# Macaron Mamba block: z's products in a stream of their own, one PSUM bank and one gate per token tile, buffers and ranks set anew

## The chip, the cores and the metric

The kernel runs on one NeuronCore of a Trainium2 chip. The metric is the time of one execution on the device in microseconds (us); the engines are TensorE (PE), VectorE (DVE), ScalarE (ACT), GpSimd (POOL) and SyncE (SP, which here only issues DMAs). All times are of this core.

## The reference

x holds 4096 tokens of 1024 channels in float32. Three residual steps follow each other: half a feed-forward layer with a ternary weight, a Mamba layer, and the same feed-forward layer again.

```python
def _L0_ffn_ref(x, weight, bias):
    scale = jnp.mean(jnp.abs(weight))
    w_t = jnp.clip(jnp.round(weight / (scale + EPS)), -1.0, 1.0)
    w_ste = weight + jax.lax.stop_gradient(w_t * scale - weight)
    return jnp.einsum('bsi,oi->bso', x, w_ste) + bias

def _mamba(x, W_in, conv_w, conv_b, W_xproj, W_dt, b_dt, A_log, Dskip, W_out):
    u, z = jnp.split(x @ W_in.T, 2, axis=-1)
    up = jnp.pad(u, ((0, 0), (K - 1, 0), (0, 0)))
    u = jax.nn.silu(conv_b + sum((conv_w[:, k] * up[:, k:k + L, :] for k in range(K))))
    x_dbl = u @ W_xproj.T                      # 64 for dt, 16 for B, 16 for C
    dt = jax.nn.softplus(dt_r @ W_dt.T + b_dt)
    # for each token: h = exp(dt * A) * h + dt * B * u ;  y = sum over the 16 states of h * C
    y = (y + u * Dskip) * jax.nn.silu(z)
    return y @ W_out.T

x = x + 0.5 * _L0_ffn_ref(_layernorm(x), weight, bias)
x = x + _mamba(_layernorm(x), ...)
x = x + 0.5 * _L0_ffn_ref(_layernorm(x), weight, bias)
```

## The kernel before

**Tiling.** The tokens go through in 16 chunks (`NC`) of 256 (`T`), each of two token tiles of 128 (`TT`). The 1024 channels are 8 blocks of 128; a half is four blocks, and the recurrence handles a chunk half by half: 32 halves, each with a skip term (n = -1) and 16 states (n = 0 to 15). That makes 544 "products", of which 512 come from VectorE.

**One state.** GpSimd multiplies u·dt by the state's B (line 934, a tile h) and adds the entering state to the first column (941). ScalarE makes the decays exp(dt·A), four instructions of 255 columns (913), into two PSUM tiles da. VectorE runs two scans over 512 columns (966), then multiplies by C (978, a tile p). TensorE sums over the states: eight transposes of 128 columns that accumulate p into the PSUM tile y (998). y is one tile of two banks, one for each token tile, and there is one such tile (line 210). After the 16th state the gate (1015) multiplies the whole of y by silu(z) on VectorE, 1024 columns at once, and only then can the next half's skip term be summed into y.

**One chunk.** `front` is one sequential generator: load x, feed-forward (`ffn`: layer norm, transposes 425, products with the ternary weight split in two parts 497, residual 476), layer norm, u's products (629), convolution and silu (574, 581), the product with W_xproj (641), `delta` of the first half (710, softplus 722), and then the next chunk. z's products (677) stand in `rest`, behind `delta` of the second half. `back` does the rest of a chunk: transposes of the gated y (752), W_out (760), residual (731), and the second feed-forward layer. `last` is `back` for the last chunk. Weights of u, z and W_out stream through five buffers; each of these streams asks for some of them ahead (`ahead`: 2, 3 and 3).

**What sets the order.** The order on every engine is made when the program is built. Each piece of work is a Python generator, a stream with a rank, that yields wishes (engine, duration, earliest time). The loop in `Streams.run` gives the instruction to the stream that can start first, and to the lower rank in a tie. The durations are constants in the code; the chip then executes each engine's queue strictly in that order, waiting on semaphores. So ranks (`DECAY`, `ENTER`, ... in lines 57 and 58), assumed latencies (`ADDED` for the bias DMA, 5000 ns for a weight) and numbers of buffers change the order of instructions, and so which engine waits for which. The eight PSUM banks are three free ones (`banks`), three for decays (`decays`) and the two of y.

Of the kernel before, what the change touches and what calls it, by code (L numbers as in the profile page):

```python
# [38 lines left out]
P = 128  # L39
# [13 lines left out]
REACH = 160  # L53
ISSUE, ADDED = 950, 6000
SWITCH = 1300

DECAY, ENTER, SUM, PREPARE, RECUR, GATE = 5, 1, 1, 0, 2, 2
FFN_A, NORM, U_PART, CONV, DELTA, OUT, FFN_C = 0, 0, 3, 0, 0, 2, 3

# [114 lines left out]
def macaron_mamba_kernel(  # L174
# [34 lines left out]
    decays = buffers(3, [P, 2, T], "da", pool_=psum)  # L209
    ys = buffers(1, [P, TT, OH], "y", pool_=psum)  # L210
    xs = buffers(6, [P, D], "x")
    xts = buffers(2, [P, NB, T], "xT")
# [128 lines left out]
    def streamed(load, n, ahead, rank):  # L341

        queue = []

        def fill():
            for i in range(n):
                yield lambda: 0 if len(queue) < ahead else INF
                w = yield from weights.take()
                load(i, w)
                queue.append((order.now + 5000, w))  # L350

        order.spawn(fill(), rank)
        return queue
# [26 lines left out]
    def stats(c, at, tiles=range(TT)):  # L380
# [4 lines left out]
        rstd, shift, less = ln[:, 28:30][:, some], ln[:, 32:34][:, some], ln[:, 36:38][:, some]  # L385
        xn = {}
        for t in tiles:
            xn[t] = yield from tmps.take()
# [50 lines left out]
    def ffn(c, which, rank, at, tiles=range(TT)):  # L439
# [32 lines left out]
        def residual(t, cols, pf, at_):  # L472
# [3 lines left out]
            nc.vector.scalar_tensor_tensor(xt, pf, hscl, xt, ALU.mult, ALU.add)  # L476
            if (*key, t) != ("a", 0, 1):
                banks.put(pf, end)
            ready["ffn", key, t, cols.start] = end
# [35 lines left out]
    def as_weights_come(key, parts, residual, rank):  # L515

        for t in range(TT):
            yield from when("parts", key, t)
        y = yield from ys.take()
        groups = {(1, h): y[:, h, :] for h in range(2)}  # L520
        for h in range(2):
            groups[0, h] = yield from banks.take()
        for k in range(NB):
            yield from when("wf", k)
# [12 lines left out]
        for t in range(TT):  # L537
            los.put(parts[t][0], end)
            his.put(parts[t][1], end)
        for h in range(2):  # L540
            end = yield from when("ffn", key, 1, h * OH)
        ys.put(y, end)

# [40 lines left out]
    def front():  # L584
        for c in range(NC):
# [32 lines left out]
            for pair in range(NB // 2):  # L618
# [4 lines left out]
                for j in range(2):  # L623
# [9 lines left out]
                    weights.put(w, end)  # L633
            yield DELTA
            px = yield from banks.take()
            for half in range(2):
                at = yield from when("u", c, half)
                end = yield pe(2 * HB * T * FULL)
                for b in range(HB):
                    k = half * HB + b  # L640
                    nc.tensor.matmul(
                        px[:NXD, :T], wx[:, k, :], u[c, half][:, b, :], start=(k == 0), stop=(k == NB - 1)
                    )
            xd[c] = yield from xds.take()
            end = yield act(T, end + REACH)
            nc.scalar.copy(xd[c][RANK:NXD, 1, :], px[RANK:NXD, :T])
            for j in range(2):
                end = yield act(T)
                nc.scalar.copy(xd[c][j * RANK : (j + 1) * RANK, 0, :], px[:RANK, :T])
            banks.put(px, end)  # L650
            bc_dram[c] = dram.tile([NST, 2, T], F32, tag="bc", name=f"bcd_{c}")
            for j in range(2):
                part_ = slice(RANK + j * NST, RANK + (j + 1) * NST)
                nc.sync.dma_start(bc_dram[c][:, j, :], xd[c][part_, 1, :])
            ready["bc", c] = end + 2500
# [80 lines left out]
    def turned(c, half, yT):  # L736
# [188 lines left out]
    def enter():  # L925
        for c, half, n in items:
# [61 lines left out]
    def summed():  # L988
        for c, half, n in items:
            yield from when("product", c, half, n)  # L990
            if n < 0:
                y = yield from ys.take()
            p = product.pop((c, half, n))
            end = yield pe(D * TURN)

            for t in range(TT):
                for b in range(HB):
                    nc.tensor.matmul(  # L998
                        y[:, t, b * P : (b + 1) * P],
                        p[:, b, t * P : (t + 1) * P],  # L1000
                        ident,
                        start=(n < 0 and b == 0),
                        stop=(n == NST - 1 and b == HB - 1),
                        is_transpose=True,
                        skip_group_check=True,
                    )
            products.put(p, end)
            if n + 1 == NST:
                order.spawn(gate(c, half, y, end + REACH), GATE)

    def gate(c, half, y, at):
        yield from when("z", c, half)
        z = sz[c, half]
        end = yield dve(1170, at)
        nc.vector.tensor_tensor(flat(z), flat(y), flat(z), ALU.mult)
        ys.put(y, end + REACH)
        ready["gate", c, half] = end + REACH

# [80 lines left out]
```

## Time and profile before

| what | value |
|---|---|
| median of 3 runs | 2726.5 us (2725.86 to 2727.03) |
| the profiled execution | 2725.84 us |
| its span, first to last instruction | 2724.1 us |
| mean granted TensorE clock | 0.983 |
| PE busy | 2568.1 us (94%) |
| DVE busy | 2288.3 us (84%) |
| ACT busy | 2001.4 us (73%) |
| POOL busy | 1815.6 us (67%) |
| DMA | 410.82 MB, mean 151 GB/s |

Busy is the time in which an engine has at least one instruction in work. Matmuls overlap in TensorE's pipeline: eight transposes that follow each other begin 0.87 us after the eight before them began, though each is listed with some 0.27 us. A float32 matmul with 256 columns is listed as two records, one transpose or one product of the feed-forward layer as one. The granted clock is the share of its pulses that TensorE was let have; it is below 1 where TensorE was idle before. An idle engine is named with the instruction that ended its wait.

### The profile page before, as it was taken

What the parts mean: (1) busy time and instruction counts of PE and PEld (TensorE: products, weight loads), DVE (VectorE), ACT (ScalarE), POOL (GpSimd) and SP (SyncE); (2) the same over time, 40 slices, a digit from 0 to 9 for tenths busy, and PEclk for the clock granted to TensorE, in tenths of its full rate; (3) what the DMA queues carried; (4) which work ended last, traced back from release to release, by engine and by line L of the source; (5) the groups of instructions that cost most, each with busy time, mean ns of one, the idle gap of its engine ahead of it and who ended that gap; (6) DMA issues with size and microseconds to landing.
All of it is one profiled execution on the core that took longest, in us unless ns stands there. A gap on an engine that the chain in (4) does not pass through costs nothing. (4 is left out here: it accounts for less than half of the span.)

```text
span 2724.1 us, 41050 instructions
## 1 busy us (share of the span) xinstructions
PE 2568.1 (94%) x14082; PEld 2199.6 (81%) x14082; DVE 2288.3 (84%) x2404; ACT 2001.4 (73%) x4202; POOL 1815.6 (67%) x1657
## 2 busy tenths in 40 slices
PE   5797989999999999999999999999999999999988
PEld 4686878888788787888878788887888878788866
DVE  4498898978899798888879799898889879788883
ACT  3678677787877778777787877778787777877662
POOL 0367767766677585767757577686767857577761
PEclk9897999999999999999999999999999999999999
DMA  4443536455454545546554454655545554554533
GB/s 158 146 130 103 168 106 216 132 166 149 134 173 140 179 151 153 155 129 184 166 162 144 140 167 132 182 162 155 153 140 167 159 172 146 150 157 133 182 85 109
DMA packets 218553, 410.82 MB, mean 151 GB/s; under 512 B 19172, under 2 KB 85860, under 8 KB 218344
## 3 DMA queue, kind: packets, MB, share of 16 engines
q1 hardware_dynamic: 209128, 374.65, 43.3%
q0 software_dynamic: 9216, 33.56, 6.8%
q8 instruction: 110, 1.80, 0.3%
q14 instruction: 99, 0.81, 0.1%
HBM read 390.82 MB, written 17.31 MB: 150 GB/s over the span
## 5 line engine op out<-in xcount | busy, mean ns | idle before, releaser
L934 POOL TENSOR_TENSOR h<-u,bc 128x1024 f32<-128x1024 f32 x512 | 1223.2, 2389 | 421.7 <-ACT da L913 171.1
L966 DVE TENSOR_TENSOR_SCAN h<-da,h 128x512 f32<-128x512 f32 x1024 | 1207.7, 1206 | 125.6 <-ACT da L913 99.7
L913 ACT ACTIVATE da<-dt,pr 128x255 f32<-128x255 f32 x2048 | 938.6, 473 | 61.9 <-DVE h L966 32.9
L978 DVE TENSOR_TENSOR p<-h,bc 128x1024 f32<-128x1024 f32 x512 | 658.7, 1286 | 6.6 <-PE y L998 6.4
L998 PE MATMUL y<-ident,p 128*128 128x128 f32 x4352 | 572.5, 278 | 79.5 <-DVE p L978 61.1
L998 PEld LDWEIGHTS y<-ident,p 128*128 128x128 f32 x4352 | 503.9, 143 | 151.5 <-DVE p L978 95.4
L629 PE MATMUL bank<-xT,weight 128*128 128x256 f32 x2048 | 474.7, 382 | 11.4 <-ACT u L562 8.6
L677 PE MATMUL bank<-weight,xT 128*128 128x256 f32 x2048 | 474.7, 380 | 9.2 <-DMA weight<-in_w_in 9.2
L760 PE MATMUL bank<-weight,u 128*128 128x256 f32 x2016 | 467.3, 381 | 2.2 <-DMA weight<-in_w_out 1.9
L629 PEld LDWEIGHTS bank<-xT,weight 128*128 128x128 f32 x2048 | 378.6, 190 | 69.9 <-ACT u L562 21.3
L677 PEld LDWEIGHTS bank<-weight,xT 128*128 128x128 f32 x2048 | 380.2, 191 | 56.7 <-ACT da L913 9.9
L760 PEld LDWEIGHTS bank<-weight,u 128*128 128x128 f32 x2016 | 370.9, 191 | 47.2 <-DMA weight<-in_w_out 2.1
L949 ACT COPY state<-h 128x4 f32<-128x4 f32 x512 | 99.2, 194 | 292.5 <-DVE h L966 287.5
L941 POOL TENSOR_TENSOR h<-h,over 128x4 f32<-128x4 f32 x512 | 262.5, 513 | 25.2
L497 PE MATMUL bank<-wf,lo 128*128 128x512 f32 x976 | 252.3, 400 | 3.7 <-DVE lo L455 2.4
L574 DVE SCALAR_TENSOR_TENSOR u<-up,pr,u 128x256 f32<-128x256 f32 x384 | 206.4, 570 | 55.2 <-ACT u L562 42.6
L497 PE MATMUL bank<-wf,hi 128*128 128x512 f32 x976 | 245.8, 394 | 0.0
L497 PEld LDWEIGHTS bank<-wf,lo 128*128 128x128 f32 x976 | 177.7, 188 | 48.4 <-issue 4.0
L497 PEld LDWEIGHTS bank<-wf,hi 128*128 128x128 f32 x976 | 181.7, 188 | 43.0 <-issue 4.3
L865 POOL TENSOR_TENSOR over<-pr,dt 128x64 f32<-128x64 f32 x32 | 24.9, 778 | 211.3 <-ACT dt L722 211.3
L476 DVE SCALAR_TENSOR_TENSOR x<-bank,hscl,x 128x512 f32<-128x512 f32 x124 | 91.2, 737 | 71.9 <-PE bank L497 71.8
L425 PE MATMUL bank<-ident,tmp 128*128 128x128 f32 x756 | 115.9, 285 | 27.1 <-ACT tmp L409 23.4
(98 smaller groups left out, 2125.0 us busy)
## 6 DMA issues: line engine op xcount, KB each, us to landing
bc<-bcd SPq DMA_DIRECT2D x512, 256.0 KB, 3.7
weight<-in_w_out SPq DMA_DIRECT2D x128, 512.0 KB, 5.1
weight<-in_w_in SPq DMA_DIRECT2D x128, 512.0 KB, 3.7
weight<-in_w_in SPq DMA_DIRECT2D x256, 256.0 KB, 4.2
x<-hbias POOLq DMA_DIRECT2D x64, 512.0 KB, 7.9
x<-in_x SPq DMA_DIRECT2D x32, 512.0 KB, 7.3
out<-x SPq DMA_DIRECT2D x30, 512.0 KB, 4.9
weight<-in_w_ffn SPq DMA_DIRECT2D x5, 512.0 KB, 7.4
```

Of the source, the lines that this page charges most:

```text
L425: nc.tensor.matmul(pt[:, j * P : (j + 1) * P], xn[:, k * P : (k + 1) * P], ident, start=(j == 0), stop=(j == 3), is_transpose=True, skip_g ...
L497: nc.tensor.matmul(pf, x[:, k, :], wf[:, k, cols], start=(x is lo and k == 0), stop=(x is hi and k == NB - 1),)
L574: nc.vector.scalar_tensor_tensor(ub, up[:, k : k + T], tap, ub, ALU.mult, ALU.add)
L629: nc.tensor.matmul(pp[:, j, :], wt[:, k, :], xT[:, k, :], start=(k == 0), stop=(k == NB - 1))
L677: nc.tensor.matmul(pp[:, t, :], xT[:, k, t * P : (t + 1) * P], wt[:, :, i, :], start=(k == 0 and t == 0), stop=(k == NB - 1), skip_group_c ...
L760: nc.tensor.matmul(po[:, t, :], yT[:, b, t * P : (t + 1) * P], wt[:, b, :], start=(half == 0 and t == 0 and b == 0), stop=(half == 1 and b ...
L913: nc.scalar.activation(da[:, i, 1:], dt[c, half][:, b, 1:], AF.Exp, scale=a_neg[:, half * HB + b, n : n + 1],)
L934: nc.gpsimd.tensor_tensor(h, u[c, half], bc[:, 0:1, :].to_broadcast([P, HB, T]), ALU.mult)
L941: nc.gpsimd.tensor_tensor(h[:, :, 0], h[:, :, 0], over[c, half][:, :, n], ALU.add)
L966: nc.vector.tensor_tensor_scan(rows_, flat(da), rows_, 0.0, ALU.mult, ALU.add)
L978: nc.vector.tensor_tensor(p, h, bc[:, 1:2, :].to_broadcast([P, HB, T]), ALU.mult)
L998: nc.tensor.matmul(y[:, t, b * P : (b + 1) * P], p[:, b, t * P : (t + 1) * P], ident, start=(n < 0 and b == 0), stop=(n == NST - 1 and b = ...
```

## The change

z's products leave the stream that followed both calls of `delta`: a stream `gates` is spawned as soon as u's products are issued, and the work from W_xproj to `delta` becomes a stream `steps` beside it, so that `front` goes on to the next chunk's feed-forward layer at once. y becomes two tiles of one bank each, taken, summed, gated and released per token tile; the gate is two instructions of 512 columns in place of one of 1024, and the transposes after it wait for their token tile's gate alone. Buffers: x 6 to 7, sz 3 to 2, p 3 to 4, bc 5 to 6; weights asked for ahead: u 2 to 3, W_out 3 to 2. `stats` takes both its tiles at once. Assumed latencies and ranks are set anew. The amount of computation stays the same, and so does every other instruction's shape.

```diff
-ISSUE, ADDED = 950, 6000
+ISSUE, ADDED = 950, 9000
+LATE_E = 700
-DECAY, ENTER, SUM, PREPARE, RECUR, GATE = 5, 1, 1, 0, 2, 2
-FFN_A, NORM, U_PART, CONV, DELTA, OUT, FFN_C = 0, 0, 3, 0, 0, 2, 3
+DECAY, ENTER, SUM, PREPARE, RECUR, GATE = 5, 2, 1, 0, 5, 5
+FFN_A, NORM, U_PART, CONV, DELTA, OUT, FFN_C = 0, 1, 3, 1, 0, 2, 3
...
-    ys = buffers(1, [P, TT, OH], "y", pool_=psum)
-    xs = buffers(6, [P, D], "x")
+    ys = buffers(TT, [P, OH], "y", pool_=psum)
+    xs = buffers(7, [P, D], "x")
-    szs = buffers(3, [P, TT, OH], "sz")
+    szs = buffers(2, [P, TT, OH], "sz")
-    products = buffers(3, [P, HB, T], "p")
-    bcs = buffers(5, [P, 2, T], "bc")
+    products = buffers(4, [P, HB, T], "p")
+    bcs = buffers(6, [P, 2, T], "bc")
...
-                queue.append((order.now + 5000, w))
+                queue.append((order.now + 6500, w))
...
-        xn = {}
+        xn = yield from tmps.take(len(tiles))
+        xn = dict(zip(tiles, xn if len(tiles) > 1 else [xn]))
...
-            queue = streamed(u_weights, NB, 2, U_PART)
+            queue = streamed(u_weights, NB, 3, U_PART)
...
-            yield DELTA
-            px = yield from banks.take()
...
-            yield from delta(c, 0, end + REACH)
-            order.spawn(rest(c, xT), DELTA)
-
-    def rest(c, xT):
-        yield from delta(c, 1, 0)
+            order.spawn(gates(c, xT), Z[0])
+            order.spawn(steps(c), DELTA)
+
+    def steps(c):
+        for half in range(2):
+            yield from when("u", c, half)
+            if not half:
+                px = yield from banks.take()
...
+        for half in range(2):
+            yield from delta(c, half, end + REACH)
         xds.put(xd[c], order.now + 2000)
+
+    def gates(c, xT):
         queue = streamed(z_weights, NB, 3, Z[0])
...
-        yield from when("gate", c, half)
         for t in range(TT):
+            yield from when("gate", c, half, t)
...
-            queue = streamed(lambda i, w: out_weights(i // 2, i % 2, w), NB, 3, OUT)
+            queue = streamed(lambda i, w: out_weights(i // 2, i % 2, w), NB, 2, OUT)
...
-                xs.put(x_tiles.pop((c, t)), order.now + 6000)
+                xs.put(x_tiles.pop((c, t)), order.now + 0)
...
-            ready["enter", c, half, n] = end + REACH
+            ready["enter", c, half, n] = end + REACH + LATE_E
...
-            if n < 0:
-                y = yield from ys.take()
-            end = yield pe(D * TURN)
             for t in range(TT):
+                if first:
+                    y[t] = yield from ys.take()
+                end = yield pe(OH * TURN)
...
+                if n + 1 == NST:
+                    order.spawn(gate(c, half, t, y[t], end + REACH), GATE)
...
-        z = sz[c, half]
-        end = yield dve(1170, at)
-        nc.vector.tensor_tensor(flat(z), flat(y), flat(z), ALU.mult)
+        z = sz[c, half][:, t, :]
+        end = yield dve(650, at)
+        nc.vector.tensor_tensor(z, y, z, ALU.mult)
```

The first chunk's feed-forward layer, which used the two banks of y beside two free banks, now takes the two tiles one after the other and gives them back with the others.

More of the change, by code (lines that the diff above doesn't have):

```diff
@@ L385, in stats @@
         rstd, shift, less = ln[:, 28:30][:, some], ln[:, 32:34][:, some], ln[:, 36:38][:, some]
-        xn = {}
+        xn = yield from tmps.take(len(tiles))
+        xn = dict(zip(tiles, xn if len(tiles) > 1 else [xn]))
         for t in tiles:
-            xn[t] = yield from tmps.take()
             end = yield act(D + 210, at[t])
@@ L476, in residual @@
             nc.vector.scalar_tensor_tensor(xt, pf, hscl, xt, ALU.mult, ALU.add)
-            if (*key, t) != ("a", 0, 1):
-                banks.put(pf, end)
+            (ys if (*key, t) == ("a", 0, 1) else banks).put(pf, end)
             ready["ffn", key, t, cols.start] = end
@@ L518, in as_weights_come @@
             yield from when("parts", key, t)
-        y = yield from ys.take()
-        groups = {(1, h): y[:, h, :] for h in range(2)}
+        groups = {}
         for h in range(2):
             groups[0, h] = yield from banks.take()
+            groups[1, h] = yield from ys.take()
         for k in range(NB):
@@ L539, in as_weights_come @@
             his.put(parts[t][1], end)
-        for h in range(2):
-            end = yield from when("ffn", key, 1, h * OH)
-        ys.put(y, end)
     u, sz, dt, xd, bc_dram, over = {}, {}, {}, {}, {}, {}
@@ L633, in front @@
                     weights.put(w, end)
-            yield DELTA
-            px = yield from banks.take()
[L636 to L654, printed above, removed]
@@ L655, in front @@
-            ready["bc", c] = end + 2500
-            yield from delta(c, 0, end + REACH)
-            order.spawn(rest(c, xT), DELTA)
-    def rest(c, xT):
-        yield from delta(c, 1, 0)
+            order.spawn(gates(c, xT), Z[0])
[5 more added lines that the diff above has]
+                px = yield from banks.take()
+            end = yield pe(2 * HB * T * FULL)
+            for b in range(HB):
+                k = half * HB + b
+                nc.tensor.matmul(
+                    px[:NXD, :T], wx[:, k, :], u[c, half][:, b, :], start=(k == 0), stop=(k == NB - 1)
+                )
+        xd[c] = yield from xds.take()
+        end = yield act(T, end + REACH)
+        nc.scalar.copy(xd[c][RANK:NXD, 1, :], px[RANK:NXD, :T])
+        for j in range(2):
+            end = yield act(T)
+            nc.scalar.copy(xd[c][j * RANK : (j + 1) * RANK, 0, :], px[:RANK, :T])
+        banks.put(px, end)
+        bc_dram[c] = dram.tile([NST, 2, T], F32, tag="bc", name=f"bcd_{c}")
+        for j in range(2):
+            part_ = slice(RANK + j * NST, RANK + (j + 1) * NST)
+            nc.sync.dma_start(bc_dram[c][:, j, :], xd[c][part_, 1, :])
+        ready["bc", c] = end + 2500
+        for half in range(2):
+            yield from delta(c, half, end + REACH)
@@ L990, in summed @@
             yield from when("product", c, half, n)
-            if n < 0:
-                y = yield from ys.take()
+            first = n < 0
+            if first:
+                y = {}
             p = product.pop((c, half, n))
-            end = yield pe(D * TURN)
             for t in range(TT):
+                if first:
+                    y[t] = yield from ys.take()
+                end = yield pe(OH * TURN)
                 for b in range(HB):
                     nc.tensor.matmul(
-                        y[:, t, b * P : (b + 1) * P],
+                        y[t][:, b * P : (b + 1) * P],
                         p[:, b, t * P : (t + 1) * P],
                         ident,
-                        start=(n < 0 and b == 0),
+                        start=(first and b == 0),
                         stop=(n == NST - 1 and b == HB - 1),
@@ L1006, in summed, with gate @@
                     )
+                if n + 1 == NST:
+                    order.spawn(gate(c, half, t, y[t], end + REACH), GATE)
             products.put(p, end)
-            if n + 1 == NST:
-                order.spawn(gate(c, half, y, end + REACH), GATE)
-    def gate(c, half, y, at):
+    def gate(c, half, t, y, at):
         yield from when("z", c, half)
-        z = sz[c, half]
-        end = yield dve(1170, at)
-        nc.vector.tensor_tensor(flat(z), flat(y), flat(z), ALU.mult)
+        z = sz[c, half][:, t, :]
+        end = yield dve(650, at)
+        nc.vector.tensor_tensor(z, y, z, ALU.mult)
         ys.put(y, end + REACH)
-        ready["gate", c, half] = end + REACH
+        ready["gate", c, half, t] = end + REACH
     for rank, gen in (
```

## The prediction

> **What bounds the kernel now.** I read the page's table of engines and the granted clock first, then TensorE's waits (all, and those from 500 to 2500 us), then windows of 10 us where it starves, then its timeline, and last the order of the two built programs. TensorE is busy for 94% of the span, and from 500 to 2500 us it waits 50 us in all:
>
> ```profile
> PE 2568.1 (94%) x14082; PEld 2199.6 (81%) x14082; DVE 2288.3 (84%) x2404; ACT 2001.4 (73%) x4202; POOL 1815.6 (67%) x1657
> PEclk9897999999999999999999999999999999999999
> ```
>
> ```profile
> PE y L998 <- DVE p L978: 21.6, 31, 1.3
> PE y L998 <- DVE sz L1015: 14.5, 11, 1.3
> PE bank L752 <- DVE x L476: 9.3, 11, 0.8
> ```
>
> The columns are us in total, times, longest. Three waits recur once or more per chunk: for a product, for the one y that the gate has not freed, for a bank that line 476 has not drained. The early slices are different:
>
> ```profile
> 200.00:210.00 10.00, 9.02 (x49) 7.48 (x48) 9.96 (x14) 7.30 (x19) 7.32 (x9) 1.00 0.33 91
> 210.00:220.00 10.00, 5.20 (x24) 4.13 (x23) 10.00 (x11) 7.04 (x13) 8.10 (x6) 0.66 0.18 61
> 220.00:230.00 10.00, 3.54 (x22) 2.53 (x20) 3.69 (x4) 8.65 (x19) 3.03 (x3) 0.84 0.47 134
> 230.00:240.00 10.00, 5.90 (x24) 4.70 (x24) 10.00 (x10) 9.41 (x22) 9.62 (x7) 0.50 0.23 81
> 240.00:250.00 10.00, 8.49 (x41) 7.76 (x42) 9.73 (x10) 7.87 (x16) 9.07 (x10) 0.64 0.50 98
> ```
>
> After the window and its length come PE, PEld, DVE, ACT, POOL busy and the clock: TensorE is half idle at a half to two thirds of its clock while DVE is full. The timeline shows why: from 209 to 243 us nothing but sums (998) and small pieces stand in its queue, each behind its product:
>
> ```profile
> 109.97 9.19 PE L677 MATMUL bank<-weight,xT 128*128 128x256 f32 x32 [9.17 <-DMA weight<-in_w_in]
> ...
> 212.73 1.65 PE L998 MATMUL y<-ident,p 128*128 128x128 f32 x8 [2.30 <-DVE p L978]
> ...
> 230.25 1.97 PE L998 MATMUL y<-ident,p 128*128 128x128 f32 x8 [6.70 <-DVE p L978]
> 233.81 1.97 PE L998 MATMUL y<-ident,p 128*128 128x128 f32 x8 [1.60 <-DVE p L978]
> ```
>
> **TensorE's account.** At full clock the timeline of 1500 to 1545 us gives, start to start, 0.87 us for eight transposes (lines 998, 425, 752), 1.73 for eight records of 256 columns, 1.83 for eight products of line 497. Times the counts of the instruction groups (4352 + 1024, 6400, 2048), with some 50 us for line 710, the work is W = 2490 us in either program. The span of 2724 holds 234 us of "loss" (idle, slow clock, refilling the pipeline). I laid W along the order of the queue and read the time at each place. The loss is 58 us at W = 60 (118 us), 88 at W = 180 (268), 107 at W = 420 (527), 195 at W = 2340 (2535), 234 at the end. So: start 107, of it some 30 in the stall shown above and 10 in a second one near 400 us; steady 88, about 7 per chunk; tail 39.
>
> **The change, part by part.**
>
> *z's stream and the start.* Before, the first chunk's z stands behind `delta`, its weights behind the loads of B and C on SP's queue, and TensorE waits the 9.17 us above. After, the order has those weights on SP ahead of B and C, z's first 16 instructions (of 64) around the first `delta`, and the next chunk's transposes and feed-forward (8 x 1.83 = 14.6 us) ahead of the first product. That also queues 12 ScalarE instructions of the next chunk (statistics, casts) ahead of the first decay. I price that from the timeline's rows (1.04 to 1.18 us for 1024 columns, 0.59 a cast, 1.28 a table load): first scan at about 111 us, not 104; first product 116, not 113. The same rows cost before 4 us of waits after the first product (statistics between decays), so the two are level by the fourth product, near 130 us.
>
> What decides is how many products TensorE asks for by a given amount of work. At W = 158 to 160, before the third chunk's feed-forward, it has summed 30 groups before and 20 after; at product 24 it has done 30 us more other work than before. So the stall of 209 to 247 us is filled, but DVE then leads: from product 4 to 60 its queue holds 240 us of work (scan 1.14, product 1.22, start to start) in both orders. Before, this took 130 to 400 us, 30 over the work: waits for ScalarE's decays (6.3 in one) and products slowed to 1.4 to 2.2 us. I give after 258: product 60 at 388, where W is 307 after and 303 before, loss 81 against 97. After that 36 us of TensorE work lie between products 60 and 64, 14 before, which covers the second stall. Start after: 107 - 26 + 2 = 83. Bounds: 97 if ScalarE's delay stays whole, 72 if DVE runs at its work alone.
>
> *One bank and one gate per tile.* Before, in every second half, 0.4 us of TensorE work covers a gate of
>
> ```profile
> L1015 DVE TENSOR_TENSOR sz<-y,sz 128x1024 f32<-128x1024 f32 x32 | 39.0, 1218 | 13.6 <-ACT sz L696 7.8 <-PE y L998 5.1
> ```
>
> After, 2.2 and 14.7 us stand there, and tile 0 needs only its own gate: 14.5 us go. The cost is 32 more VectorE instructions. No row has this shape; its neighbours of 512 columns out of PSUM take 677 (455) and 737 ns (476), so a gate costs 2 x 677 - 1218 = 136 to 2 x 737 - 1218 = 256 ns more: 4 to 8 us, hidden in VectorE's 436 us of idle; in the two stretches where DVE leads, three halves, under 1 us.
>
> *Order, ranks, buffers in the steady part.* For each result that VectorE takes from TensorE and puts ahead of a product, the margin is the TensorE work between that result and the sum of the product, less the VectorE work between. Before, one of the eight residuals (476) per chunk has -1.2 us: 12.8 us over eleven chunks, of the 21.6 seen. After, none is negative; the least are 0.5 to 0.7. A bank is taken again under 1 us after a feed-forward product in 23 of 100 cases before, in none after (least 1.3, a drain takes 0.74): 9.3 us go. A weight buffer's least gap between uses grows from 5.2 to 6.9 us of work (a weight lands in 3.7 to 5.1). So 12.8 + 14.5 + 9.3 = 36.6 us can go. Margins of half a microsecond do not hold against products that took 1.20 to 2.20 us, so I take half, 18: steady 70. Bounds: 88 (all comes back) and 50 (all go, with their refills).
>
> *Tail.* From product 480 to 512 the order has 124 us of VectorE work and 103 of TensorE's; it took 139 before with 123 and 108. I take 134. After: loss at product 480 is 83 + 70 - 2 = 151 at W = 2355, so 2506; the last sum at 2640, W = 2458; behind it 32 us of work (40 before, in 49 us), with the same 9 to 10 of waits, 42. Span 2682, tail 39 to 41: the tail gives nothing back. Its bounds are 139 in place of 134 and 124 + 4.
>
> *At nothing:* `LATE_E`, `ADDED` and 6500 are only the planner's beliefs; the bias lands after 7.9 us where 6 was assumed. They act through the order counted above. The later gate (rank 5) is covered by the 2.2 and 14.7 us.
>
> Sum: 2490 + 83 + 70 + 39 = 2682; the execution was 1.7 us over its span and 0.7 under the median, so 2684; with 2 for the margins' start-up I say 2686.
>
> [...] In the windows above the clock is 0.50 at 230 to 240 us, though the gaps there are 1.6 to 1.7 us. [...]
>
> **Rivals.** (1) *VectorE sets the pace everywhere.* For: before, TensorE's sum begins within 1 us of its product's end nearly throughout. Then TensorE only does other work earlier (21 us earlier per product in the steady part), the last product ends where it did, at 2675 with 4 us more work and the 6.3 us wait for a decay gone, and 42 follow: 2673 + 42 = 2715. Against: VectorE has 16% idle, TensorE 2.5% between 500 and 2500 us.
> (2) *The steady waits come back elsewhere*: the change then does its work at the start alone, 2686 + 18 = 2704. For: margins of 0.5 us. Against: they are all positive.
> (3) *The recurrences pay for their lower rank* (RECUR 2 to 5, ENTER 1 to 2). Where DVE leads, products 4 to 60 and 480 to 512, some 92 states, every foreign instruction let in ahead goes to the end. One of 0.74 us each is 68 us: 2686 + 68 = 2754; it is slower than before from 0.44 each (40 us). For: ranks and `LATE_E`. Against: VectorE's work up to products 60 and 512 is 258 and 2250 us after, 258 and 2246 before.
>
> **Chances.** Forecast 0.68, its own range 2662 to 2704; (2) 0.10; (1) 0.13; (3) 0.09. What can be told from no change here is 0.2%, 5 us. (1) lies across that bound: 0.08 faster, 0.05 same. So faster 0.68 + 0.10 + 0.08 = 0.86, same 0.05, slower 0.09. The range goes down to the low bounds together (2686 - 11 - 20 + 7 = 2662) and up past (1), to 2721.
>
> **What would show it.** TensorE not half idle in 210 to 250 us and no wait on z's weights near 110; the first scan some 7 us later; waits for the gate and for line 476's bank gone; waits for products from 500 to 2500 us under 15 us; about 42 us behind the last sum. Wrong if product 60 lands after 400 us, or if the loss per chunk is still 7.

## The result, and the profile after

The median of 13 runs is 2717.2 us (2712.9 to 2725.2), beside 2726.3 us for 13 runs of the kernel before (2724.1 to 2728.9): a ratio of 0.9971, 95% interval 0.9962 to 0.9980. The change makes the kernel 9 us faster; 40 were forecast. The profiled execution, on which the sums below stand, has a span of 2711.1 us and is the fastest of the 13.

The page's engine totals and granted clock, in the order of those shown of before:

```profile
PE 2559.0 (94%) x14082; PEld 2196.0 (81%) x14082; DVE 2277.4 (84%) x2436; ACT 1990.1 (73%) x4195; POOL 1743.9 (64%) x1657
PEclk9989799999999999999999999999999999999989
```

The work is the same and 32 VectorE instructions are new. The slice of lowest clock has moved on by one: it is the fifth, 271 to 339 us at 67.8 us a slice. TensorE's waits from 500 to 2500 us (us in total, times, longest):

```profile
PE bank L627 <- ACT u L560: 12.1, 13, 0.9
PE bank L498 <- DVE x L478: 8.2, 11, 0.8
PE bank L427 <- ACT tmp L411: 7.4, 11, 0.7
PE bank L627 <- ACT up L557: 5.5, 12, 0.5
PE y L1003 <- DVE p L980: 4.1, 13, 0.3
```

Of the three waits of before, the one for a product falls from 21.6 to 4.1 and the one for the gate (14.5) is not among these rows. The one for a bank that the residual has not drained stays: 9.3 before, 8.2 now, the residual being line 478 here and the wait standing at line 498. New are 25 us of waits for ScalarE: for its pieces of the convolution (560, 557) and its normalised tiles (411). The gate's group (busy, mean ns, idle before it):

```profile
L1020 DVE TENSOR_TENSOR sz<-y,sz 128x512 f32<-128x512 f32 x64 | 41.1, 674 | 15.0 <-PE y L1003 15.0
```

Against 39.0 us in 32 instructions before: 2 us more busy time (4 by the means, whose records overlap), and no wait of TensorE from 500 to 2500 us is for it. The start, in windows of 10 us (PE, PEld, DVE, ACT, POOL busy, clock, DMA share, GB/s):

```profile
210.00:220.00 10.00, 10.00 (x54) 8.18 (x54) 3.85 (x4) 7.91 (x13) 5.02 (x7) 1.00 0.35 114
220.00:230.00 10.00, 7.44 (x38) 5.38 (x37) 3.87 (x5) 9.04 (x18) 3.43 (x3) 1.00 0.70 159
230.00:240.00 10.00, 10.00 (x45) 8.19 (x45) 10.00 (x12) 5.45 (x14) 5.25 (x4) 1.00 0.15 52
...
260.00:270.00 10.00, 2.44 (x10) 2.04 (x11) 7.66 (x7) 7.75 (x18) 3.81 (x3) 0.63 0.07 26
270.00:280.00 10.00, 6.80 (x32) 5.35 (x30) 10.00 (x9) 6.07 (x16) 9.63 (x6) 0.51 0.24 79
280.00:290.00 10.00, 3.30 (x20) 2.43 (x16) 8.33 (x8) 9.54 (x21) 6.71 (x7) 0.66 0.17 52
290.00:300.00 10.00, 3.91 (x16) 3.14 (x16) 10.00 (x10) 4.84 (x13) 8.38 (x6) 0.50 0.23 62
```

The old stall (210 to 250 us) is filled, but while TensorE is busy there, VectorE stands still for more than half of 210 to 230 us; and from 260 to 300 us TensorE starves as it did before at 209 to 247. The stall was not removed but moved. Its rows in TensorE's timeline (start, length, what it waited for):

```profile
265.96 1.97 PE L1003 MATMUL y<-ident,p 128*128 128x128 f32 x8 [6.43 <-DVE p L980]
269.53 1.97 PE L1003 MATMUL y<-ident,p 128*128 128x128 f32 x8 [1.60 <-DVE p L980]
```

Why VectorE stood still is in its own timeline:

```profile
145.04 1.22 DVE L968 TENSOR_TENSOR_SCAN h<-da,h 128x512 f32<-128x512 f32 x1 [7.50 <-ACT da L915]
...
223.25 1.42 DVE L457 TENSOR_TENSOR lo<-bank,hi 128x512 fp32r<-128x512 f32 x2 [9.40 <-ACT hi L455]
...
261.13 1.22 DVE L968 TENSOR_TENSOR_SCAN h<-da,h 128x512 f32<-128x512 f32 x1 [6.31 <-ACT da L915]
```

and what ScalarE did in the meantime, in ScalarE's (208 to 228 us, some rows):

```profile
210.17 1.28 ACT L579 ACT_TABLE_LOAD   x1
211.47 1.06 ACT L579 ACTIVATE u<-u 128x1024 f32<-128x1024 f32 x1
...
216.20 0.36 ACT L649 COPY xd<-bank 32x256 f32<-32x256 f32 x1 [1.67 <-PE bank L644]
...
217.37 2.37 ACT L411 ACTIVATE tmp<-x,ln 128x1024 f32<-128x1024 f32 x2
219.76 1.28 ACT L724 ACT_TABLE_LOAD   x1
...
222.63 1.31 ACT L455 CAST hi<-bank 128x512 fp32r<-128x512 f32 x2
...
227.81 3.71 ACT L915 ACTIVATE da<-dt,pr 128x255 f32<-128x255 f32 x8
```

From 206 to 228 us ScalarE works through one long stretch without a decay: statistics, normalised tiles and casts of the third chunk, and of the second chunk u's silu, the copies of x_dbl (for which it waits for TensorE) and softplus. Behind it, in the same queue, stand the casts that VectorE needs at 223 us and the decays that it needs at 228. Counted by the scans, two a state, these decays are for state 20 of the first chunk's 32, and the three rows above at 145, 223 and 261 us all lie before that chunk's last product. Its dt had long been there; the second half's was made at 128 us:

```profile
128.02 1.57 ACT L724 ACTIVATE dt<-bank,pr 128x256 f32<-128x256 f32 x4
```

So the decays did not wait for dt; they waited for their turn in ScalarE's queue.

With the prediction's own account (loss = time less TensorE's work W at full clock, read at W = 420 and 2340), this is where 13 us of the profiled span came from:

| loss in us | before | forecast | after |
|---|---|---|---|
| start (to W = 420) | 107 | 83 | 122 |
| steady (420 to 2340) | 88 | 70 | 59 |
| tail | 39 | 39 | 40 |
| span = 2490 + the three | 2724 | 2682 | 2711 |

29 us won in the steady part, 15 lost at the start where 24 were to be won.

### The profile page after: what moved, and what is told of

It reads as the page before. It is cut to its first block, busy times and chain, and to the rows that moved or that the text cites. A ratio compares the mean times of both kernels' runs of the same rounds, so it can differ in the third digit from the quotient of the medians.

```text
span 2711.1 us, 40943 instructions
## 1 busy us (share of the span) xinstructions
PE 2559.0 (94%) x14082; PEld 2196.0 (81%) x14082; DVE 2277.4 (84%) x2436; ACT 1990.1 (73%) x4195; POOL 1743.9 (64%) x1657
## 4 chain that ended last, share of the span: by engine, by line
PE 56%; DVE 12%; ACT 8%; issue 6%; DMA 5%; POOL 3%; SPq 0%; DVEq 0%; POOLq 0%; ACTq 0%
PE bank L762 15%; PE bank L627 14%; PE y L1003 11%; PE bank L679 6%; PE bank L498 6%; DVE h L968 6%; DVE p L980 4%; ACT da L915 2%; DMA out<-x 2%; DMA x<-in_x 2%; PE bank L427 2%; POOL h L936 1%; DVE u L572 1%; DMA bc<-bcd 1%; DVE x L478 1%
## 5 line engine op out<-in xcount | busy, mean ns | idle before, releaser
L980 DVE TENSOR_TENSOR p<-h,bc 128x1024 f32<-128x1024 f32 x512 | 679.7, 1328 | 0.2
L1003 PEld LDWEIGHTS y<-ident,p 128*128 128x128 f32 x4352 | 510.4, 144 | 125.0 <-DVE p L980 66.5
L679 PEld LDWEIGHTS bank<-weight,xT 128*128 128x128 f32 x2048 | 373.9, 191 | 44.4 <-ACT dt L724 0.8
L943 POOL TENSOR_TENSOR h<-h,over 128x4 f32<-128x4 f32 x512 | 240.4, 470 | 28.4
L572 DVE SCALAR_TENSOR_TENSOR u<-up,pr,u 128x256 f32<-128x256 f32 x384 | 174.1, 498 | 88.2 <-ACT u L560 74.3
L394 POOL TENSOR_SCALAR ln<-ln 128x1 f32<-128x1 f32 x96 | 76.2, 794 | 104.5 <-ACT tmp L392 100.7
L427 PEld LDWEIGHTS bank<-ident,tmp 128*128 128x128 f32 x756 | 92.3, 146 | 59.2 <-ACT tmp L411 38.4
```

Source lines behind the costliest of these rows:

```text
L427: nc.tensor.matmul(pt[:, j * P : (j + 1) * P], xn[:, k * P : (k + 1) * P], ident, start=(j == 0), stop=(j == 3), is_transpose=True, skip_g ...
L572: nc.vector.scalar_tensor_tensor(ub, up[:, k : k + T], tap, ub, ALU.mult, ALU.add)
L679: nc.tensor.matmul(pp[:, t, :], xT[:, k, t * P : (t + 1) * P], wt[:, :, i, :], start=(k == 0 and t == 0), stop=(k == NB - 1), skip_group_c ...
L943: nc.gpsimd.tensor_tensor(h[:, :, 0], h[:, :, 0], over[c, half][:, :, n], ALU.add)
L980: nc.vector.tensor_tensor(p, h, bc[:, 1:2, :].to_broadcast([P, HB, T]), ALU.mult)
L1003: nc.tensor.matmul(y[t][:, b * P : (b + 1) * P], p[:, b, t * P : (t + 1) * P], ident, start=(first and b == 0), stop=(n == NST - 1 and b = ...
```

## The experiments

Each was timed against the kernel before. The medians are of 2 to 13 runs (2 in c1 and c2, 3 in c3 and i, 4 in a1 to a4, b1, d2 and d3), and the loss at the start and in the steady part comes from one profile each: for after that of its fastest run, for i the fastest of 3 (2700.8 us), for h2 the slowest of 8 (2725.4). Two profiles of one order of instructions differ: a kernel whose edit leaves after's queues almost as they are (h2 below, the norm's numbers constant) shows 127 at the start and 66 in the steady part beside after's 122 and 59. Differences under some 7 us in these columns are not used.

| kernel | median us | ratio to before, 95% | start | steady |
|---|---|---|---|---|
| after | 2717.2 | 0.9971 (0.9962 to 0.9980) | 122 | 59 |
| a1 split y alone, on before | 2790.2 | 1.0235 (1.0218 to 1.0252) | 118 | 139 |
| a2 streams alone, on before | 2801.9 | 1.0277 (1.0262 to 1.0293) | 108 | 126 |
| a3 after with the old ranks | 2804.7 | 1.0291 (1.0275 to 1.0306) | 132 | 140 |
| a4 after with one y and one gate | 2773.6 | 1.0178 (1.0163 to 1.0194) | 116 | 126 |
| b1 after, front waits for steps | 2736.3 | 1.0040 (1.0025 to 1.0055) | 108 | 104 |
| b2 the same in chunks 0 and 1 only | 2722.4 | 0.9990 (0.9980 to 0.9999) | 114 | 82 |
| b3 the same in chunk 1 only | 2725.2 | 0.9998 (0.9989 to 1.0007) | 115 | 76 |
| b4 b2 and the old ranks at the start | 2718.8 | 0.9978 (0.9969 to 0.9988) | 116 | 68 |
| c1 after without table loads | 2707.5 | 0.9927 (0.9907 to 0.9947) | 117 | 61 |
| c2 before without table loads | 2701.1 | 0.9904 (0.9884 to 0.9924) | 104 | 69 |
| c3 after, norm on 8 columns early | 2712.8 | 0.9954 (0.9938 to 0.9969) | 118 | 62 |
| c4 before, norm on 8 columns early | 2723.4 | 0.9993 (0.9982 to 1.0003) | 106 | 86 |
| d1 after, decays first in chunk 0 | 2733.5 | 1.0023 (1.0013 to 1.0033) | 139 | 64 |
| d2 the same in chunks 0 and 1 | 2835.4 | 1.0399 (1.0385 to 1.0413) | 134 | 172 |
| d3 before, the same in chunks 0 and 1 | 2740.2 | 1.0049 (1.0035 to 1.0062) | 121 | 87 |
| h1 d1, norm's numbers constant early | 2729.8 | 1.0010 (1.0000 to 1.0020) | 140 | 64 |
| h2 after, norm's numbers constant early | 2717.7 | 0.9965 (0.9955 to 0.9975) | 127 | 66 |
| i all of c1, c3 and h2 on after | 2710.5 | 0.9936 (0.9894 to 0.9978) | 112 | 57 |

### The parts alone (a1 to a4)

a1 and a4 put the two one-bank tiles of y and the gate per tile into before, or take them out of after; a2 gives before the streams `gates` and `steps` alone; a3 keeps after but for the ranks.

```diff
# a1, on before (a4 is the reverse, on after)
-    ys = buffers(1, [P, TT, OH], "y", pool_=psum)
+    ys = buffers(TT, [P, OH], "y", pool_=psum)
...
# a2, on before
-            yield from delta(c, 0, end + REACH)
-            order.spawn(rest(c, xT), DELTA)
+            order.spawn(gates(c, xT), Z[0])
+            order.spawn(steps(c), DELTA)
...
# a3, on after
-DECAY, ENTER, SUM, PREPARE, RECUR, GATE = 5, 2, 1, 0, 5, 5
-FFN_A, NORM, U_PART, CONV, DELTA, OUT, FFN_C = 0, 1, 3, 1, 0, 2, 3
+DECAY, ENTER, SUM, PREPARE, RECUR, GATE = 5, 1, 1, 0, 2, 2
+FFN_A, NORM, U_PART, CONV, DELTA, OUT, FFN_C = 0, 0, 3, 0, 0, 2, 3
```

Expected of a1:

> The kernel before with one part of the change: y as two tiles of one bank, one gate per token tile; streams, ranks and buffers as before. By the prediction's step the 14.5 us of waits for the gate between 500 and 2500 us go and nothing else: loss from 420 to 2340 us from 88 to about 74, time 2710 to 2716. If the parts only work together, the loss there stays 85 or more and the time is 2722 or more.

Expected of a2:

> The kernel before with the streams alone: z's products spawned behind u's, the work from W_xproj to delta beside them, the front stream going on at once; one y, ranks and buffers as before. By Theory A2 the start is as in the changed kernel or worse: group 60 of the sums at 400 us or later (386 before), loss at 420 us of work 115 to 130. In the steady part, if the streams alone are enough, the loss from 420 to 2340 us is 55 to 75; if ranks and the split y are needed, 88 or more, as in the two kernels without them (126 and 140), time 2740 or more.

Expected of a3:

> The changed kernel with the two lines of ranks as they were before (RECUR 2, ENTER 1, GATE 2, NORM and CONV 0); all else changed. Theory A: the start keeps its loss, 118 to 126 us at 420 us of work, since the front stream still runs ahead; time within 8 us of 2717 or worse, with what the steady part does to it. Theory B: loss at 420 falls to 100 to 110 and the time to 2698 to 2706.

Expected of a4:

> The changed kernel with y as one tile of two banks and one gate of 1024 columns again; all else changed. If the steady gain of 29 us comes half from the gate, the waits of the sums for the gate are back at 12 to 18 us between 500 and 2500 us, the loss from 420 to 2340 us rises from 59 to 71 to 77, time 2727 to 2735. If the gain comes from the order alone, the loss stays near 59 and the time within 5 us of 2717.

Measured: each of these two parts alone makes the kernel slower (by 64 and 76 us), and after without its ranks or its split y is slower too (by 87 and 56 against after). None of the steady losses that were forecast for single parts came out (a1 about 74, a2 55 to 75, a4 59 or 71 to 77); a1 and a2 show the alternative written beside them, that the parts only work together. a2's start of 108 is below the 115 to 130 expected, and its tail, not in the table, is 75 us (2799.0 of span less 2490, 108 and 126) where before has 39. Splitting the gate shortens the wait for it: from 500 to 2500 us TensorE's waits for it are 14.5 us before, 6.6 in a1, 0.7 in a3. But the waits come back under other names. a3's, with the old ranks:

```profile
PE bank L712 <- DVE x L478: 20.9, 11, 1.9
PE bank L627 <- ACT u L560: 19.5, 21, 0.9
PE bank L427 <- ACT sz L693: 13.4, 11, 1.2
PE y L1003 <- DVE p L980: 8.8, 9, 1.1
```

and a4's, with one y:

```profile
PE y L1007 <- DVE sz L1024: 17.1, 4, 5.5
PE y L1007 <- DVE p L984: 15.2, 15, 4.6
PE bank L427 <- ACT tmp L411: 14.2, 8, 10.0
```

TensorE's idle time from 540 to 2540 us is 56 us before, 41 after, and 74 to 83 in these four. What follows: these parts do not add up. One planner orders all queues, so each edit gives another order of everything, and none of the parts tried carries the steady gain alone. The numbers of buffers were not tried by themselves.

### Holding the next chunk back (b1 to b4)

The prediction said that the next chunk's work, pulled ahead, fills the first stall. These put the steps back into the way of `front`, everywhere or at the start.

```diff
             order.spawn(gates(c, xT), Z[0])
-            order.spawn(steps(c), DELTA)
+            yield DELTA
+            yield from steps(c)
```

b2 does so for c < 2, b3 for c == 1; b4 adds to b2 the old ranks (and no `LATE_E`) for the first two chunks, the first three for the convolution and the norm.

Expected of b1:

> The changed kernel with the front stream waiting for both calls of delta in every chunk; z's stream, gate, ranks and buffers stay. Theory A for the start: loss at 420 us of work 100 to 110. If running ahead is what makes the steady part better, the loss from 420 to 2340 us rises from 59 towards 88, time 2715 to 2730; if it does nothing there, it stays near 59 and the time is 2698 to 2706.

Expected of b2:

> The changed kernel, but for the first two chunks the front stream waits for both calls of delta before it goes on to the next chunk, as before; z's stream, the split gate, ranks and buffers stay, and the order from the third chunk on is the changed one. Theory A (the start lost what the steady part won because, with VectorE setting the pace, the next chunk's statistics, normalisation and casts stand on ScalarE ahead of the decays): TensorE's loss at 420 us of work falls from 122 us to 100 to 110, the loss from there to 2340 us stays near 59, time 2698 to 2706. Theory B (the lower ranks of the recurrence lose the start): loss at 420 stays 118 to 125, time 2713 to 2722.

Expected of b3:

> The changed kernel with the front stream waiting for delta in chunk 1 alone: the order is the changed one up to product 16 and again from chunk 2 on; in between the third chunk's feed-forward layer stands behind delta. By Theory E the loss at 180 us of work stays at 67 as in the changed kernel and the 40 us it lost from 180 to 240 shrink: loss at 240 of 80 to 98, at 420 of 98 to 113, time 2695 to 2710. If the passage between orders costs what it did where two chunks waited (32 us from 420 to 900 in place of 15), the time is 2712 to 2725.

Expected of b4:

> The changed kernel with the ranks of before and the waiting front stream in the first two chunks (conv and norm ranks in the first three), and the changed order from then on: an attempt at the start of before with the steady part of after. If both keep what they had alone, the loss at 420 us of work is 104 to 112, that from 420 to 2340 is 59 to 65, and the time 2700 to 2710. If the passage from one order to the other costs as much as when only the streams were held back (32 us from 420 to 900), the time is 2716 to 2726.

Measured: with `front` held back everywhere, the start is before's again (108), and 45 us of the steady part are lost: in this order running ahead is worth 45 in the steady part and costs 14 at the start. Held back at the start alone, the loss at W = 180 is up (99 to 102 in b1 to b4, 67 after) and by W = 420 it is 114 to 116. At W = 240 it is 101 to 103 in these and 107 after: the start is paid for earlier or later. b3's loss at W = 180 was to stay at 67, and the losses at 420 that would have shown a cure (98 to 113) were reached by b1 alone. b4 is level with after (2718.8, intervals overlap), nothing is better.

What running ahead does to VectorE shows in its idle time between its first and its 60th product: 31 us before, 51 after. a2, which gives before the two streams and nothing else, has 55. With `front` held back it is 41 in b1 and b2 and 46 in b3 and b4. So the streams by themselves bring the whole of the extra wait, and holding back `front` takes about half of it away; in b1 and b2, 14 us of their 41 lie ahead of the fourth product, where after has under 1.

### How much ScalarE has to do (c1 to c4)

If the length of such stretches on ScalarE were the cause, less work in them would shorten the start. c1 and c2 compute silu as a copy and softplus as exp, so that no table is loaded again; c3 and c4 let the layer norm's statistics, its normalisation and the casts of the feed-forward layer work on 8 of their columns in chunks 1 to 3.

```diff
# c1, on after; c2, on before
-            nc.scalar.activation(flat(u[c, half]), flat(u[c, half]), AF.Silu)
+            nc.scalar.activation(flat(u[c, half]), flat(u[c, half]), AF.Identity)
...
# c3, on after; c4, on before
-                nc.scalar.copy(part_hi, pt)
+                nc.scalar.copy(part_hi[:, few(c)], pt[:, few(c)])
```

Expected of c1:

> The changed kernel with silu left out (its input is copied) and softplus replaced by exp, so that ScalarE needs one function table; the order on every engine is the changed kernel's, less some 173 table loads of 1.28 us on ScalarE. Theory A2 (the start is paced by VectorE's products, and those by what stands ahead of the decays on ScalarE): VectorE's waits for ScalarE between products 4 and 64 fall from some 40 us to under 25, group 64 of the sums begins at 398 to 408 us in place of 423, the loss at 420 us of work falls from 122 to 97 to 110. [...]

Expected of c2:

> The kernel before with the same left out: silu a copy, softplus an exp, one table, order otherwise its own. Its VectorE waited 26 us in the start where the changed kernel's waited 50, so by Theory A2 it gains less there: loss at 420 us of work from 107 to 95 to 103, group 64 at 390 to 398 us in place of 403. [...]

Expected of c3:

> The changed kernel, order kept, but in chunks 1 to 3 ScalarE's statistics, normalisations and casts of the layer norms handle 8 columns in place of 1024 or 512 (the rest of those tiles keeps older data): some 6 to 7 us less of ScalarE's work in each norm. Theory A3 (in the start the run of the next chunk's work on ScalarE between two groups of decays is what VectorE waits for): VectorE's idle time from product 4 to group 64 falls from 50 to 25 to 35 us, group 64 begins at 395 to 408 us in place of 423, the loss at 420 us of work is 98 to 110 in place of 122. Theory C (VectorE's own pace): group 64 at 418 or later, loss at 420 at 116 or more.

Expected of c4:

> The kernel before with the same columns left out in chunks 1 to 3. Its decays were interleaved with that work, so by Theory A3 it gains less: group 64 at 392 to 400 us in place of 403, loss at 420 at 95 to 104 in place of 107. By Theory C: 403 and 107 within 4.

Measured: c1 takes 173 table loads and 224 us of ScalarE's work away (1990.1 to 1766.1 busy) and the start is 117 in place of 122; in c3 it is 118, and neither is clear of the 7 us. VectorE's idle time from product 4 to group 64 of the sums (product 60; four groups are skip terms) is 49.8 us after, 46.9 in c1, 45.3 in c3; before has 26.2. So the amount of ScalarE's work is a small part of it. Theory C, that VectorE's own work sets the pace, has the start's loss that it named in c3 and c4 (118 and 106), but not its reason: VectorE is busy for 239 us of that stretch after and for 244 before, and idle for the rest.

### The decays first (d1 to d3), and the norm's numbers (h1, h2)

If it is the place of the decays behind such a stretch, a lower rank for them should help.

```diff
+            yield 0 if c < 1 else DECAY      # d1; c < 2 in d2 and d3
             yield from when("dt", c, half)
```

h1 and h2 write constants where GpSimd worked out the norm's numbers in chunks 1 to 3 (0 for the mean, 1 for the scale), so that GpSimd no longer waits for ScalarE's statistics:

```diff
+        if 0 < c < 4:
+            nc.gpsimd.memset(rstd, 1.0)
+            nc.gpsimd.memset(shift, 0.0)
+            return ln, xn, end + REACH
```

Expected of d1:

> The changed kernel with the decays of chunk 0 at rank 0 in place of 5, so that in a tie on ScalarE they go ahead of the next chunk's work; nothing else is edited, and from chunk 1's products on the order is the changed kernel's. Theory A4 (VectorE's extra waits in the start come from the place of the decays: ties give ScalarE to the next chunk's statistics, dt and casts, which themselves wait for TensorE and GpSimd, and the decays stand behind that chain): VectorE's idle time from product 4 to group 64 falls from 50 to 25 to 40 us, the loss at 240 us of work from 107 to 85 to 98, at 420 from 122 to 100 to 114, the later loss stays at 59, time 2700 to 2712. Theory D (the chain from u's convolution to dt is as long wherever the decays stand, and the start cannot be shortened by ScalarE's order): loss at 420 stays 117 or more, time 2714 to 2722.

Expected of d2:

> As the first of these, with chunks 0 and 1 at rank 0; the order after that settles a little differently from the changed kernel's. Theory A4: loss at 420 us of work 95 to 112, time 2696 to 2712 if the later loss stays near 59. Theory D: loss at 420 at 117 or more.

Expected of d3:

> The kernel before with the decays of chunks 0 and 1 at rank 0; from there on its own order. Theory A4: it had 26 us of such idle time, so it gains less: loss at 420 us of work 107 to 92 to 103, time 2712 to 2722. Theory D: loss at 420 within 4 of 107, time 2723 to 2730.

Expected of h1:

> The kernel with the decays of chunk 0 first, order kept, but in chunks 1 to 3 the small numbers of the layer norms (mean, 1/deviation) are constants, so that GpSimd does not wait for ScalarE's statistics. Theory E (each in-order queue of the start carries pieces of the next chunk's norm, which wait for another engine, and whichever piece stands ahead of a state's h, decay or scan sets VectorE's wait): VectorE's waits for h, 32 us from product 4 to group 64, fall under 12, its idle time from 55 to 22 to 38, the loss at 420 us of work from 139 to 108 to 122. Theory D (the chain from u's convolution to dt limits the start whatever stands on GpSimd): loss at 420 at 130 or more.

Expected of h2:

> The changed kernel, order kept, with the same constants in chunks 1 to 3. Its VectorE waits for decays and casts of ScalarE, whose queue also waits for TensorE; so by Theory E the loss at 420 us of work falls little, from 122 to 112 to 119; more than that (under 110) would put the whole of the start's loss on the norm's numbers.

Measured: the wait for the decays goes, and another takes its place; none of the gains written for these five kernels came, and h1's waits for h, which were to fall under 12 us, are 30. Theory D, that the chain to dt limits the start, has its loss in d1, d2 and h1, but in after the row at 128 us above speaks against it: the first chunk's decays were late with their dt at hand. VectorE's waits from 130 to 430 us, after first:

```profile
DVE h L968 <- ACT da L915: 26.0, 7, 7.5
DVE lo L457 <- ACT hi L455: 10.2, 3, 9.4
...
DVE h L968 <- POOL h L943: 3.1, 2, 1.7
```

d1:

```profile
DVE h L969 <- POOL h L944: 31.4, 5, 11.7
DVE lo L457 <- ACT hi L455: 7.4, 3, 6.0
...
DVE h L969 <- ACT da L916: 2.6, 2, 1.9
```

Now h from GpSimd is late. In d1 GpSimd's next instruction was one of the norm, which needs ScalarE's statistics (the row names the copy of the state behind them; the statistics end at 145.7 us, the copy at 145.8), and with the norm's numbers made constant GpSimd stands as long behind ScalarE's copy of the state, which frees its buffer. The row of each in GpSimd's timeline, d1:

```profile
145.80 0.21 POOL L394 TENSOR_SCALAR ln<-ln 128x1 f32<-128x1 f32 x1 [13.38 <-ACT state L952]
```

h1:

```profile
147.59 2.35 POOL L944 TENSOR_TENSOR h<-u,bc 128x1024 f32<-128x1024 f32 x1 [13.51 <-ACT state L959]
```

In both edits the item that VectorE needs, directly or through GpSimd, stands behind a stretch on ScalarE. d1 is not a clean test of the decays' place, though: with them in between, softplus and exp alternate, and ScalarE loads a table 182 times in place of 174, some 10 us more at 1.28 each, all in the start. d2 spreads this into the steady part (172); before suffers as well (d3, 121).

### All of it at once (i)

After's order with c1, c3 and h2 together: silu a copy, softplus exp, 8 columns and constant norm numbers in chunks 1 to 3.

Expected of i:

> The changed kernel, its order kept, with ScalarE relieved of three things at once: no table is loaded (silu is a copy, softplus an exp), the layer norm's two statistics, its normalisation and the hi casts of chunks 1 to 3 work on 8 columns, and the norm's numbers of those chunks are constants. ScalarE's queue stands in the same order, so the decays and state copies stay behind the same items, which now take little. Theory A (what ScalarE has to do in its runs sets the start): the decay and state waits go, TensorE's loss at 420 us of its work falls from 122 to 110 or less, VectorE's idle between products 4 and 60 from 50 to some 30 us, time 2690 to 2700. Theory B (the run on ScalarE waits itself, for TensorE and for banks, and hands the wait on whatever it has to do): loss 115 or more, time 2703 to 2710, near the two kernels that took away one or the other.

Measured: 2710.5 us (2700.8 to 2714.6), start 112, VectorE's idle time from product 4 to group 64 42.1 us (49.8 in after). ScalarE's busy time falls to 1710.1 us, and its waits rise. From 130 to 300 us, after:

```profile
ACT state L951 <- DVE h L968: 23.8, 16, 3.0
ACT up L557 <- PE bank L627: 7.2, 6, 2.6
ACT u L560 <- PE bank L627: 2.1, 1, 2.1
...
```

and this kernel:

```profile
ACT state L961 <- DVE h L978: 35.6, 22, 3.0
ACT up L567 <- PE bank L637: 9.3, 7, 2.6
ACT xT L608 <- PE bank L437: 9.2, 3, 5.8
...
```

Where ScalarE has less to do it waits longer for TensorE's banks and for scans instead, and what is queued behind goes on waiting. The median is next to theory B's 2703 to 2710, and the start's 112 lies between the two theories. VectorE's idle time falls by 7.7 us, about what c1 (2.9) and c3 (4.5) took together: that is a third of the 23.6 us by which after exceeds before. So ScalarE's amount of work explains some third, and the rest is not the amount.

## Why the prediction was right in sign and wrong in size

*The step that failed* is in "z's stream and the start": from product 4 to 60 "I give after 258: product 60 at 388". It took 288, from 130 to 418 us, 48 over VectorE's 240 us of work where 18 were allowed. At product 60 the loss is 111 in place of 81, 30 of the error. The next step, that the work behind product 60 covers the second stall, failed as well: from there to W = 420 the loss grows by 11 where 2 were allowed. Together they are the 39 by which the start's 122 exceeds 83; the steady part gives 11 back. The prediction had named the sign of it: wrong if product 60 lands after 400 us.

The 18 has no working beside it: the prediction gives before's 30 over its work, names ScalarE's decays as a cause, and then says 258. It counted VectorE's work up to a product, which is the same in both orders, and laid out ScalarE's only up to the fourth product. It did not follow ScalarE's queue past that point, where `front`, running ahead, sets a whole chunk's statistics, tiles, copies and tables between two groups of decays. VectorE's idle time there is 49.8 us, 46 of it in the rows below; before it was 26.2. That the streams bring this wait is shown by a2, that it stands in ScalarE's queue and not in a missing dt by the rows at 128 and 206 to 228 us. The bound of 97 was drawn as if the old order's delay were the worst one.

| VectorE's idle, product 4 to group 64, us | before | after | d1 |
|---|---|---|---|
| for decays (ScalarE) | 18.5 | 26.0 | 2.6 |
| for casts and state copies (ScalarE) | 0.8 | 14.2 | 8.4 |
| for h (GpSimd) | 1.8 | 5.8 | 32.0 |
| in all | 26.2 | 49.8 | 54.9 |

*Right by their own numbers:* z's weights are no longer waited for (the 9.17 us; the loss at W = 60 falls from 58 to 42). The fourth product is level, near 130 us in both. The stall of 209 to 247 us is filled. The split gate costs 674 ns, so 2 x 674 - 1218 = 130 ns a gate or 4 us in all, at the foot of the 4 to 8 forecast, and not waited for in the steady part. From product 480 to 512 it takes 133 us (134 forecast), 41.9 follow the last sum (42), and the tail is 40 (39).

*The second stall* was to be covered and is not: TensorE is 13.31 us busy from 420 to 440 us, and waits 5.74 us in one place, for softplus:

```profile
431.46 1.11 PE L754 MATMUL bank<-ident,sz 128*128 128x128 f32 x4 [5.74 <-ACT dt L724]
```

The loss grows by 10 us from W = 300 to 360, as by 13 before. The prediction counted TensorE's work in that place and not that a bank it needs is drained by ScalarE, whose softplus stands between the statistics of another chunk.

*The steady part:* half of 36.6 us of waits was to go, 18. TensorE's idle time from 540 to 2540 us falls from 56.3 to 41.3, 15.0. Of the named waits, those for a product and for the gate went (36.1 to about 4). The 9.3 for the residual's bank, which were to go whole, did not (8.2), and 25 us of new waits are for ScalarE, whose margins the prediction had not laid out at all: its pieces of the convolution before the bank of line 627, the normalised tiles before line 427. So the "half" is near, but by another way than the one argued, and that is luck. The loss fell by 29, of which the idle time explains 15; the rest is not in the clock either (1.00 in both from 500 to 2500 us) and was not found. In other profiles with this steady order the loss is 57 to 68, so that 59 is near the good end.

*The rivals.* (1), VectorE sets the pace, gave 2715, next to the median, but not for its reason: TensorE waits 4.1 us for products from 500 to 2500 us. VectorE leads at the start alone, and there it does not run at its work. The outer range of 2662 to 2721 holds the median only because it was stretched past this rival. (2), the steady waits come back: in part, as said. (3), the lower ranks cost: not by b4, which has the old ranks in the first two chunks and is otherwise b2, and is 3.6 us faster than b2 (2718.8 and 2722.4); with the old ranks throughout (a3) the kernel takes 2805 us. The rival's own 92 states are 88 by its bounds (56 and 32).

*The clock in the gaps.* After, the sums come every 3.57 us with gaps of 1.60 from 266 to 280 us, at a clock of 0.51 (270 to 280 us), and take 1.97 us each (1.09 where TensorE is busy). But these rows lie behind a gap of 6.43 us, as before's at 230 us lie behind 6.70: there the clock stays at half with gaps of 1.60 us (0.50 from 230 to 240 us in before), and neither row shows whether such gaps alone bring it down. Another stretch of before has no gap so long: in the window of 210 to 220 us the clock is 0.66, and the gaps there are 2.30 (the prediction's row at 212.73) and 2.50:

```profile
216.89 1.97 PE L998 MATMUL y<-ident,p 128*128 128x128 f32 x8 [2.50 <-DVE p L978]
```

How long a gap has to be to lower the clock was not tried.

*Open:* which single link sets the length of the start. Shown is that the streams bring the wait, that after's waits end on ScalarE's queue, that neither less work there, nor another rank of the decays, nor constant norm's numbers bring the start to 83, and that ScalarE in turn waits for TensorE and for scans. z's stream was not tried without `steps`. That this loop of in-order queues is the cause, and that an order written out by hand would break it, was not tried.

## What to carry to other kernels

Work pulled ahead to fill a stall of one engine also puts its instructions into every other in-order queue: lay out the queue of the engine that feeds the bottleneck (here ScalarE's, between two groups of decays) over the whole stretch, not up to its first items, before an idle gap is booked as gain. A wait taken away by a rank or by less work tends to come back under another name, so judge by the loss of a stretch and not by the wait. In a kernel ordered by a planner the parts of a change need not add up: here two of them alone cost 64 and 76 us, and the whole set won 9.

## What the runs showed that was not expected

Table loads matter more to before than to after: without them (two runs each) before falls by 25 us to 2701 and after by 10 to 2708, so that the change no longer gains (ratios 0.9904 and 0.9927, whose intervals overlap). Of before's 25 us, 19 are in the steady part, but TensorE's idle time there falls by 6 only (56.3 to 50.7); where the rest comes from was not found.

A table load takes 1.28 us and the function behind it starts 1.30 us after the load did (210.17 and 211.47): nothing further is lost in that row.

The times of after are spread over 12 us, those of before over 5; no experiment explains this.
